# An attention-and-network megakernel: loads spread over three places of a slot, one masked query moved to ScalarE, five network groups turned by 32x32 blocks ahead of time

## The chip, the cores and the metric

The kernel runs on one core of a Trainium2 chip, in float32 throughout. The metric is the time of one execution on the device in microseconds; the median of several executions is compared. TensorE (PE in the profile, its weight loads PEld) does the matrix products, VectorE (DVE) and ScalarE (ACT) the elementwise work, GpSimd (POOL) what is left of it, and SyncE (SP) issues nearly all DMA transfers, one after the other, from one queue.

## The reference, cut to what matters

There are 16 sequences of 256 tokens with 256 features, and 16 contexts of the same shape. Each sequence goes through three attentions with 16 heads of 16 features, and then a network:

```python
# layer 0: cross-attention between RMS norms
q, k, v = rms(x) @ Wq, rms(ctx) @ Wk, rms(ctx) @ Wv
x = rms(x + softmax(q k' / 4, masked) v @ Wo)
# layer 1: causal self-attention with rotary embedding, layer 2: the same, not causal, with k, v from ctx
h = layernorm(x)
q, k = rope((h @ wq + bq) / 4), rope(h @ wk + bk)
x = x + softmax(q k', causal) v @ wo + bo
# layer 3
x = x + gelu(layernorm(x) @ fc1 + b1) @ fc2 + b2      # 256 -> 1024 -> 256
```

## The kernel before

**Slots.** The 48 attentions (16 sequences x 3 layers) are done one after the other, in an order written out by hand: the digits of `ORDER` (L31) are the layers. One attention is a *slot*. Inside slot i the kernel does the scores, exponentials and value products of attention i, block by block (`scores`, L538; `values`, L574), and in between pieces of other attentions: the q, k and v projections of attention i+1, the division and projection of attention i-2, the finish of i-3, the norms of i+2. A slot of layer 0 or 2 has four blocks; a causal slot (layer 1) has three, since the part above the diagonal is left out. Which piece stands where is written out in the loop at L983 to L1102; the program records instructions in that order, and each engine runs its own in order. Semaphores are the only link between engines.

In each block PE does the scores (L551), the value products of the block before (L590) and one 256-column projection (L329 for q and k, L341 for v and for the output). PE turns without a pause if everything that it reads is there: qm and kT of the next attention at the slot's boundary, the exponentials `pt` a block later.

**q and k.** For the layers 1 and 2, `q` (L474) adds the bias on ScalarE (L461), then VectorE does a shuffle (L465), two products (L469), a sum (L485) and two products with a 0/1 mask (L487): `qm` holds q twice, once with the even heads blanked out and once with the odd ones. `k` (L505) takes the same steps and ends with the sum into `kT` (L510). In a causal slot the k of the next attention follows on VectorE right behind its q; in the others the inversion of the softmax sums stands between them.

**The way of the value products.** `take` (L604) copies them from PSUM and sends them to DRAM (`hop<-av`), once for each half. `end` (L610, in block 0 of the next slot) sends the second half and fetches the sums and the values in another layout (`sums<-hop`, `oT<-hop`). `invert` (L622, block 1) takes reciprocals on VectorE (L627), and spreads them over partitions through DRAM (`inv_hop<-sums`, `inv<-inv_hop`). `divide` (L639, block 0 of the slot after) multiplies by them (L641). All of it is issued by SP in order, so that whatever stands ahead of a transfer on SP, or waits there, holds it up.

**Loads.** A layer-0 attention needs four transfers of 256 KB (x, y and both transposed: `cur`, `y`, `xT`, `yT`), issued in the slot three before it; there are 11 such slots (i = 3, 5, 7, 11, 14, 17, 21, 24, 29, 31, 33). `load_next` (L976) issues two of them in block 0, behind the transfers of `end`, and two in block 1, behind those of `invert`. Where no layer 0 is due, one weight matrix is issued at each of the two places while there are any.

**Turning.** A normalised sequence is needed with features on partitions. Either PE does it (`turn_ps`, L282: four 128x128 transposes into PSUM, then a copy), or `pieces_out` (L431) has VectorE transpose 32x32 blocks (L436) and writes them to DRAM, and `pieces_in` (L445) reads them back in four transfers. 23 of the attentions use the second way, 9 the first; the result is `hT`, with runs of 32 tokens.

**The network.** It handles two sequences at a time: eight groups (`Mlp`, L709), each with seven products of 512 features by Strassen-like sums for the first layer (`up`) and seven for the second (`down`). The loop at L1115 interleaves `up` of group g+1 with `down` of group g, and prepares group g+2: `stats`, `norm`, `keep` (adds a bias on POOL), `turn` on PE between `down(2)` and `down(7)` (L1156), with a copy to SBUF by ScalarE (L729), and `mix` (L748, four differences on VectorE). The PSUM tile `X` of `up` is used by four products in turn, and `add_sum` (L779) has to read it before the next.

Of the kernel before, what the change touches and what calls it, by code (L numbers as in the profile page):

```python
# [8 lines left out]
F32 = mybir.dt.float32  # L9
# [64 lines left out]
def xattn_kernel(  # L74
# [217 lines left out]
    def turned(src):  # L292
# [7 lines left out]
        return t  # L300

    def all_tokens(src, k, like=None):

        if len(src.shape) == 3:
            return src[:, k], like
        if like is not None:
            like = like.rearrange("p (c q i) -> p c q i", c=NC, i=32)
        return src[:, :, k].rearrange("p q c i -> p c q i"), like
# [40 lines left out]
    class Att:  # L349
# [81 lines left out]
        def pieces_out(self):  # L431

            self.norm()
            t = work.tile([P, 4, KC, NC, 32], F32, tag="a", name="turn")
            for k in range(KC):
                nc.vector.transpose(  # L436
                    t[:, :, k].rearrange("p g c i -> p c g i"),
                    self.xn[:, :, k * P : (k + 1) * P].rearrange("p c (g j) -> p c g j", j=32),
                )
            self.turn_hop = dram.tile([P, 4, KC * NC * 32], F32, tag="turn", name="turn_hop")  # L440
            nc.sync.dma_start(
                out=self.turn_hop, in_=t.rearrange("p g k c i -> p g (k c i)")
            )

        def pieces_in(self):  # L445

            self.hT = turn_tile()
            hop = self.turn_hop.rearrange("(q j) g f -> g j q f", j=32)
            for g in range(4):
                nc.sync.dma_start(  # L450
                    out=self.hT[32 * g : 32 * g + 32].rearrange("p q k c i -> p q (k c i)"),
                    in_=hop[g],
                )
            self.kvT = self.hT if self.layer == 1 else yTs[self.b]
# [18 lines left out]

        def q(self):  # L474
            ps = by_feature(self.hT, self.w, 0)
            self.qm = work.tile([P, KC, 2, S], F32, tag="qm", name="qm", bufs=2)
            if self.layer == 0:
                rq = self.rq.unsqueeze(1).to_broadcast([P, KC, S])
                for i in range(2):
                    nc.vector.scalar_tensor_tensor(  # L480
                        self.qm[:, :, i, :], ps, parity[i], rq, ALU.mult, ALU.mult
                    )
                return
            a, u = self.rotated(ps, 0)
            nc.vector.tensor_tensor(a, a, u, ALU.add)  # L485
            for i in range(2):
                nc.vector.tensor_scalar(self.qm[:, :, i, :], a, parity[i], None, ALU.mult)  # L487

# [220 lines left out]
    class Mlp:  # L709
# [11 lines left out]
        def keep(self):  # L721
            for x in self.xs:
                add_bias(x, R_FC2)

        def turn(self, copy=nc.scalar.copy):
            self.hT = self.pool.tile([P, KC, 2, S], F32, tag="qm", name="hT3")
            for i, xn in enumerate(self.xns):
                ps = turn_ps(xn)
                copy(self.hT[:, :, i, :], ps.rearrange("p (k s) -> p k s", s=S))  # L729

        def mix(self, tag="av", bufs=None):

            b = self.hT
            if tag == "av":
# [9 lines left out]
            for o, x, y in (  # L744
                (t1, b[:, 0, 1], b[:, 0, 0]), (t2, b[:, 1, 1], t1),
                (t3, b[:, 1, 1], b[:, 0, 1]), (t4, b[:, 1, 0], t2),
            ):
                nc.vector.tensor_tensor(o, x, y, ALU.subtract)  # L748

        def up_product(self, n, banks, a, b, first):  # L750
            for c in range(4):
                nc.tensor.matmul(  # L752
                    banks[c // 2][:, (c % 2) * S : (c % 2 + 1) * S],
                    lhsT=a[:, c * P : (c + 1) * P], rhs=b,
                    start=(first and c % 2 == 0), stop=True, skip_group_check=True,
                )
# [38 lines left out]
        def up(self, n):  # L795
            b, ts = self.hT, getattr(self, "ts", None)
            if n == 1:
                self.X = psS.tile([P, 2, 512], F32, tag="S", name="upX")
                self.X = [self.X[:, i] for i in range(2)]
                self.up_product(1, self.X, up_a(0, 0), b[:, 0, 0], True)  # L800
                self.keep_or_add(0, 0, self.X)
# [8 lines left out]
            elif n == 2:  # L810
                w = [dense_ps() for _ in range(2)]
                self.up_product(2, w, up_a(0, 1), b[:, 1, 0], True)
                self.keep_or_add(0, 0, w)
# [3 lines left out]
            elif n == 3:  # L817
                self.up_product(3, self.Z, up_s[2], b[:, 1, 1], False)
# [119 lines left out]
    with tc.manual_schedule():  # L938
# [36 lines left out]

        def load_next(i):  # L976
            n = 2 if i > 1 and ahead is not None and ahead.layer == 0 else int(i > 2)
            for t, w in due[:n]:
                nc.sync.dma_start(out=t, in_=w)
            del due[:n]  # L980

        turns = turned_ahead()
        for i in range(N_ATT):  # L983
# [4 lines left out]
            if i > 1 and ahead is not None and ahead.layer == 0:  # L988
                due[:0] = batch(ahead.b)


# [3 lines left out]
            for n in range(len(a.blocks)):  # L995
# [8 lines left out]
                if n == 0:  # L1004
# [9 lines left out]
                    do(turns.get(i - 1), "pieces_in")  # L1014
                    load_next(i)
                    if late:
# [13 lines left out]
                    if i == N_ATT - 1:  # L1030
                        mlps[0].turn(nc.vector.tensor_copy)
                        mlps[0].keep()
                    do(i + 1, "q")
                elif n == 1:

                    if a.causal:
                        do(i + 1, "k")
                    if last is not None:
# [76 lines left out]
        for g in range(B // 2):  # L1115
            this = mlps[g]
            ahead, next_but_one = (mlps[i] if i < B // 2 else None for i in (g + 1, g + 2))

# [472 lines left out]
```

## Time and profile before

| | |
|---|---|
| Median of 3 executions | 944.01 us (943.09 to 948.07) |
| Profiled execution | 935.7 us, its span 933.8 us |
| Granted TensorE clock | 0.999 |
| PE busy in the span | 920.2 us (99%) |
| DVE busy | 679.2 us (73%) |
| ACT busy | 533.2 us (57%) |
| POOL busy | 314.0 us (34%) |
| Attention, 89 to 708 us | PE 613.9 of 619 us |
| Network, 742 to 929 us | PE 186.97 of 187 us, DVE 122.49, ACT 73.62 |

Busy time of PE comes from modelled ends of pipelined products, so it is not a proof that PE runs at its peak; a delay shows best in the start of one stretch of products against the next. A row of the timeline has the start, the length, the engine with its line, the operation, output and inputs, shape and number; square brackets tell how long the engine was idle before it and what ended that. "SPq" is SP's issue of a transfer; its length is the time of issuing alone.

### The profile page before, as it was taken

The page shows a single profiled execution, that of the slowest core. Times are in us where ns is not written, and L with a number is a line of the kernel's source. Part 1 is how long each engine was busy: PE and PEld are TensorE (multiplying, and loading weights), DVE is VectorE, ACT ScalarE, POOL GpSimd, SP SyncE. Part 2 cuts the span into 40 slices and gives each one's busy share as a digit, 9 for nine tenths or more (in the row PEclk, how much of TensorE's full clock was granted, in tenths as well). Part 3 has the DMA queues.
Part 4 walks back from the last instruction along what each step waited for, and adds up shares of the span by engine and source line. Part 5 has one row for each costly group of instructions (what it writes and reads, how often), then busy time and mean ns, then how long its engine had stood idle before and what let it go on. Part 6 is the DMA issues. An engine that isn't in the chain of part 4 may idle for free.

```text
span 933.8 us, 29304 instructions
## 1 busy us (share of the span) xinstructions
PE 920.2 (99%) x12266; PEld 540.2 (58%) x12266; DVE 679.2 (73%) x1486; ACT 533.2 (57%) x749; POOL 314.0 (34%) x503
## 2 busy tenths in 40 slices
PE   8999999999999999999999999999999999999997
PEld 4444444445454544454454445455444799999997
DVE  4458677886878787868966878897887566667663
ACT  4666655766666665756656666666666634344440
POOL 4213543324444464443533434344033121122200
PEclk9999999999999999999999999999999999999999
DMA  9434454454334343432435433223222100000001
GB/s 297 155 100 126 128 170 136 132 159 125 124 106 144 94 129 98 152 111 84 141 121 157 132 106 98 90 86 102 92 76 82 36 24 23 20 4 24 24 24 48
DMA packets 115550, 95.26 MB, mean 102 GB/s; under 512 B 23498, under 2 KB 112210, under 8 KB 115410
## 3 DMA queue, kind: packets, MB, share of 16 engines
q1 hardware_dynamic: 114722, 92.77, 31.8%
q8 instruction: 98, 1.61, 0.7%
q10 hardware_dynamic: 688, 0.54, 0.2%
q14 instruction: 42, 0.34, 0.1%
HBM read 57.08 MB, written 36.20 MB: 100 GB/s over the span
## 4 chain that ended last, share of the span: by engine, by line
PE 78%; DVE 11%; DMA 5%; issue 2%; SPq 2%; POOL 2%; ACT 1%; DVEq 0%
PE S L551 15%; PE A L590 14%; PE d L341 13%; PE d L329 13%; PE upX L752 6%; PE A L850 5%; PE downZ L850 3%; PE upZ L752 3%; DVE u L469 2%; PE d L850 2%; DVE a L469 2%; PE d L752 2%; DVE u L465 1%; PE d L286 1%; DMA hop<-av 1%
## 5 line engine op out<-in xcount | busy, mean ns | idle before, releaser
L562 ACT ACTIVATE pt<-S 128x1024 f32<-128x1024 f32 x224 | 217.3, 1022 | 135.3 <-PE S L551 135.0
L551 PE MATMUL S<-qm,kT 32*128 32x512 f32 (+1 forms) x1536 | 202.8, 599 | 4.1 <-DVE kT L510 3.6
L590 PE MATMUL A<-pt,va 128*32 128x256 f32 (+1 forms) x3072 | 191.2, 367 | 1.3 <-POOL pt L569 0.7
L590 PEld LDWEIGHTS A<-pt,va 128*32 128x32 f32 x3072 | 80.5, 109 | 157.0 <-issue 92.7
L562 ACT ACTIVATE pt<-S,sy 128x1024 f32<-128x1024 f32 x128 | 135.7, 1111 | 50.8 <-PE S L551 50.5
L569 POOL TENSOR_SCALAR_AFFINE_SELECT pt<-pt 128x512 f32<-128x512 f32 x128 | 90.7, 725 | 147.5 <-ACT pt L562 146.6
L551 PEld LDWEIGHTS S<-qm,kT 32*128 32x128 f32 x1536 | 62.8, 183 | 76.0 <-issue 41.2
L317 POOL TENSOR_TENSOR cur<-cur,bias 128x512 f32<-128x512 f32 x48 | 68.7, 1438 | 56.5 <-DVE xn L271 56.5
L461 ACT ACTIVATE a<-d,qk_bias 128x256 f32<-128x256 f32 x128 | 53.8, 471 | 52.5 <-PE d L329 31.1
L329 PE MATMUL d<-hT,sa 128*32 128x256 f32 x1024 | 61.1, 379 | 0.0
L246 POOL TENSOR_SCALAR r_ln<-bmv 128x2 f32<-128x2 f32 x48 | 15.3, 318 | 118.0 <-DVE bmv L265 116.5
L469 DVE TENSOR_TENSOR u<-u,turn 128x512 f32<-128x512 f32 x64 | 52.2, 816 | 0.0
L469 DVE TENSOR_TENSOR a<-a,turn 128x512 f32<-128x512 f32 x64 | 49.8, 777 | 2.2
L641 DVE TENSOR_TENSOR oT<-oT,inv 128x512 f32<-128x512 f32 x48 | 39.2, 818 | 14.2 <-DMA inv<-inv_hop 13.0
L607 DVE COPY av<-A 128x512 f32<-128x512 f32 x47 | 32.2, 684 | 22.7 <-PE A L590 22.3
L465 DVE STREAM_SHUFFLE u<-a 128x512 f32<-128x512 f32 x64 | 47.4, 741 | 0.0
L790 ACT ACTIVATE g<-g,fb 128x256 f32<-128x256 f32 x96 | 41.0, 499 | 11.1 <-DVE g L779 11.1
L329 PEld LDWEIGHTS d<-hT,sa 128*32 128x32 f32 x1024 | 33.2, 110 | 22.0 <-issue 0.2
L246 POOL TENSOR_SCALAR r_o<-ms_o 128x2 f32<-128x2 f32 x16 | 3.9, 242 | 122.3 <-DVE sq L254 112.7
L650 DVE TENSOR_TENSOR cur<-d,cur 128x512 f32<-128x512 f32 x32 | 21.6, 676 | 29.0 <-PE d L341 29.0
L271 DVE TENSOR_SCALAR xn<-cur,bmv,r_ln 128x256 f32<-128x256 f32 x96 | 41.5, 481 | 0.8 <-POOL r_ln L247 0.8
L845 DVE TENSOR_TENSOR g<-g,g 128x512 f32<-128x512 f32 x64 | 40.9, 681 | 0.0
(148 smaller groups left out, 1556.0 us busy)
## 6 DMA issues: line engine op xcount, KB each, us to landing
hop<-av SPq DMA_DIRECT2D x96, 256.0 KB
oT<-hop SPq DMA_DIRECT2D x96, 128.0 KB
inv<-inv_hop SPq DMA_DIRECT2D x96, 128.0 KB
turn_hop<-turn SPq DMA_DIRECT2D x23, 256.0 KB
hT<-turn_hop SPq DMA_DIRECT2D x92, 64.0 KB
xT<-in_xt SPq DMA_DIRECT2D x16, 256.0 KB
cur<-in_x SPq DMA_DIRECT2D x16, 256.0 KB
yT<-in_yt SPq DMA_DIRECT2D x16, 256.0 KB
```

What stands on the lines that cost most here:

```text
L317: nc.gpsimd.tensor_tensor(t, t, bias_sb[:, row : row + D].unsqueeze(1).to_broadcast([P, NC, D]), ALU.add)
L329: nc.tensor.matmul(o, lhsT=w[:, k, at + t * P + j : at + t * P + j + 32], rhs=tokens, start=(k == 0), stop=(k == KC - 1), skip_group_check ...
L341: nc.tensor.matmul(ps[j : j + 32, c * D : (c + 1) * D], lhsT=some_tokens(src, k, c, j), rhs=w[:, k, at : at + D], start=(k == 0), stop=(k ...
L461: nc.scalar.activation(a[:, t], ps[:, t], AF.Identity, bias=bias[:, t : t + 1])
L465: nc.vector.stream_shuffle(u.rearrange("p t s -> p (t s)"), a.rearrange("p t s -> p (t s)"), SWAP)
L469: nc.vector.tensor_tensor(t, t, table.unsqueeze(1).to_broadcast([P, KC, S]), ALU.mult)
L551: nc.tensor.matmul(ps[:, j, 2 * m * u : 2 * m * (u + 1)] .rearrange("p (i s) -> p i s", i=2), lhsT=self.kT[r, t, kc * P : (kc + 1) * P], r ...
L562: nc.scalar.activation(pt[:, :, :w], ps[:, :, :w], AF.Exp, scale=scale)
L569: nc.gpsimd.affine_select(out=diag, in_=diag, compare_op=ALU.is_ge, fill=0.0, base=0, pattern=[[0, 2], [0, 2], [1, P]], channel_multiplier=-1,
L590: nc.tensor.matmul(self.av[32 * r : 32 * r + 32, i, q0:S], lhsT=self.va[:, kc, 8 * t + 2 * r + i, :], rhs=pts[r // 2][:, r % 2, i * m : (i ...
L752: nc.tensor.matmul(banks[c // 2][:, (c % 2) * S : (c % 2 + 1) * S], lhsT=a[:, c * P : (c + 1) * P], rhs=b, start=(first and c % 2 == 0), s ...
L850: nc.tensor.matmul(ps[:, c, :], lhsT=a[f // 2][:, f % 2, c * P : (c + 1) * P], rhs=b[:, f, :], start=(first and c == 0 and f == 0), stop=True,
```

## The change

It has three parts.

- `load_next` is called at three places instead of two: at the very start of a slot (ahead of the scores of block 0, so ahead of `end` on SP's queue), in block 1 behind `invert` as before, and in the last block. Where a layer 0 is due, two transfers go at the first place and one at each of the others (before: two and two). Where none is due, one weight matrix each at the first and the second (before: the same number, the first of them behind `end`).
- `q` can leave out the second of its two mask products. It does so if the current attention is causal; the product is then done by ScalarE, as an activation Copy with the mask as its scale, behind the two bias activations of k in block 1. Only next attentions of layer 1 or 2 have such a product, so that it concerns five causal slots (i = 21, 28, 38, 40, 42).
- The 32x32 way of turning becomes a pair of functions, and the network's groups 3 to 7 use it: statistics, norm and VectorE transposes of group g+3 in iteration g, writing to DRAM behind `down(3)`, and the reading back in iteration g+1. Groups 0 to 2 are turned by PE as before, now with a copy into the same layout. All products and differences that read this `hT` read it in runs of 32.

Instruction by instruction, PE loses 40 transposes and is otherwise unchanged; ScalarE loses ten copies and gains five activations; VectorE loses five mask products and gains 20 transposes, and statistics and norms move; POOL is unchanged; SP gains 10 writes and 40 reads in the network.

```diff
+    def pieces_out(xn):
+        t = work.tile([P, 4, KC, NC, 32], F32, tag="a", name="turn")
+        for k in range(KC):
+            nc.vector.transpose(
+                t[:, :, k].rearrange("p g c i -> p c g i"),
+                xn[:, :, k * P : (k + 1) * P].rearrange("p c (g j) -> p c g j", j=32),
+            )
+        hop = dram.tile([P, 4, KC * NC * 32], F32, tag="turn", name="turn_hop")
+        nc.sync.dma_start(out=hop, in_=t.rearrange("p g k c i -> p g (k c i)"))
+        return hop
+
+    def pieces_in(t, hop):
+        for g in range(4):
+            nc.sync.dma_start(
+                out=t[32 * g : 32 * g + 32].rearrange("p q k c i -> p q (k c i)"),
+                in_=hop.rearrange("(q j) g f -> g j q f", j=32)[g],
+            )
...
-        def q(self):
+        def q(self, both=True):
...
-            for i in range(2):
-                nc.vector.tensor_scalar(self.qm[:, :, i, :], a, parity[i], None, ALU.mult)
+            nc.vector.tensor_scalar(self.qm[:, :, 0, :], a, parity[0], None, ALU.mult)
+            self.rotated_q = a
+            if both:
+                nc.vector.tensor_scalar(self.qm[:, :, 1, :], a, parity[1], None, ALU.mult)
+
+        def second_mask(self):
+            if self.layer > 0:
+                nc.scalar.activation(
+                    self.qm[:, :, 1, :], self.rotated_q, AF.Copy, scale=parity[1]
+                )
...
+        def new_hT(self):
+            t = self.pool.tile([P, 2, 4, KC, NC, 32], F32, tag="qm", name="hT3")
+            self.hT = [t[:, i] for i in range(2)]
...
+        def pieces_out(self):
+            self.hops = [pieces_out(xn) for xn in self.xns]
+
+        def pieces_in(self):
+            self.new_hT()
+            for t, hop in zip(self.hT, self.hops):
+                pieces_in(t, hop)
...
-        def load_next(i):
-            n = 2 if i > 1 and ahead is not None and ahead.layer == 0 else int(i > 2)
+        def load_next(i, n, later):
+            if not (i > 1 and ahead is not None and ahead.layer == 0):
+                n = later if i > 2 else 0
...
                 due[:0] = batch(ahead.b)
+            load_next(i, 2, 1)
...
                     do(turns.get(i - 1), "pieces_in")
-                    load_next(i)
...
-                    do(i + 1, "q")
+                    if i + 1 < N_ATT:
+                        att(i + 1).q(both=not a.causal)
                 elif n == 1:
                     if a.causal:
-                        do(i + 1, "k")
+                        do(i + 1, "k", "second_mask")
...
-                    load_next(i)
+                    load_next(i, 1, 1)
...
                     do(due_turn, "turn")
+                    load_next(i, 1, 0)
...
-            if next_but_one is not None:
+            if g == 0:
                 next_but_one.stats()
             if ahead is not None:
                 ahead.ups(5, 6)
                 this.sum_a(2)
+            if g > 0 and next_but_one is not None:
+                next_but_one.keep()
+                next_but_one.pieces_in()
...
-            if next_but_one is not None:
+            if g == 0:
                 next_but_one.norm()
                 next_but_one.keep()
+            if third is not None:
+                third.stats()
...
             this.down(2)
+            if g == 0:
+                next_but_one.turn()
             if next_but_one is not None:
-                next_but_one.turn()
                 next_but_one.mix()
...
             this.down(7)
+            if third is not None:
+                third.norm()
             this.down(3)
+            if third is not None:
+                third.pieces_out()
             this.down(4)
```

More of the change, by code (lines that the diff above doesn't have):

```diff
@@ L300, in turned, with by_groups @@
         return t
+    def pieces_out(xn):
[14 more added lines that the diff above has]
+            )
+    def by_groups(t):
+        return t.rearrange("p (c q i) -> p c q i", c=NC, i=32)
     def all_tokens(src, k, like=None):
@@ L306, in all_tokens @@
         if like is not None:
-            like = like.rearrange("p (c q i) -> p c q i", c=NC, i=32)
+            like = by_groups(like)
         return src[:, :, k].rearrange("p q c i -> p c q i"), like
@@ L433, in pieces_out @@
             self.norm()
[L434 to L443, printed above, removed]
+            self.hop = pieces_out(self.xn)
         def pieces_in(self):
             self.hT = turn_tile()
[L448 to L453, printed above, removed]
+            pieces_in(self.hT, self.hop)
             self.kvT = self.hT if self.layer == 1 else yTs[self.b]
@@ L723, in keep, with part @@
                 add_bias(x, R_FC2)
+        def new_hT(self):
+            t = self.pool.tile([P, 2, 4, KC, NC, 32], F32, tag="qm", name="hT3")
+            self.hT = [t[:, i] for i in range(2)]
         def turn(self, copy=nc.scalar.copy):
-            self.hT = self.pool.tile([P, KC, 2, S], F32, tag="qm", name="hT3")
-            for i, xn in enumerate(self.xns):
+            self.new_hT()
+            for t, xn in zip(self.hT, self.xns):
                 ps = turn_ps(xn)
-                copy(self.hT[:, :, i, :], ps.rearrange("p (k s) -> p k s", s=S))
+                copy(
+                    t.rearrange("p q k c i -> p (k c) q i"),
+                    ps.rearrange("p (k q i) -> p k q i", q=4, i=32),
+                )
+        def pieces_out(self):
+            self.hops = [pieces_out(xn) for xn in self.xns]
+        def pieces_in(self):
+            self.new_hT()
+            for t, hop in zip(self.hT, self.hops):
+                pieces_in(t, hop)
+        def part(self, k, i):
+            return all_tokens(self.hT[i], k)[0]
         def mix(self, tag="av", bufs=None):
-            b = self.hT
+            b = self.part
             if tag == "av":
@@ L744, in mix @@
             for o, x, y in (
-                (t1, b[:, 0, 1], b[:, 0, 0]), (t2, b[:, 1, 1], t1),
-                (t3, b[:, 1, 1], b[:, 0, 1]), (t4, b[:, 1, 0], t2),
+                (t1, b(0, 1), b(0, 0)), (t2, b(1, 1), t1),
+                (t3, b(1, 1), b(0, 1)), (t4, b(1, 0), t2),
             ):
+                o, y = (t if len(t.shape) == 4 else by_groups(t) for t in (o, y))
                 nc.vector.tensor_tensor(o, x, y, ALU.subtract)
@@ L751, in up_product @@
             for c in range(4):
+                o = banks[c // 2][:, (c % 2) * S : (c % 2 + 1) * S]
                 nc.tensor.matmul(
-                    banks[c // 2][:, (c % 2) * S : (c % 2 + 1) * S],
+                    o if len(b.shape) == 2 else by_groups(o),
                     lhsT=a[:, c * P : (c + 1) * P], rhs=b,
@@ L795, in up @@
         def up(self, n):
-            b, ts = self.hT, getattr(self, "ts", None)
+            b, ts = self.part, getattr(self, "ts", None)
             if n == 1:
@@ L799, in up @@
                 self.X = [self.X[:, i] for i in range(2)]
-                self.up_product(1, self.X, up_a(0, 0), b[:, 0, 0], True)
+                self.up_product(1, self.X, up_a(0, 0), b(0, 0), True)
                 self.keep_or_add(0, 0, self.X)
@@ L811, in up @@
                 w = [dense_ps() for _ in range(2)]
-                self.up_product(2, w, up_a(0, 1), b[:, 1, 0], True)
+                self.up_product(2, w, up_a(0, 1), b(1, 0), True)
                 self.keep_or_add(0, 0, w)
@@ L817, in up @@
             elif n == 3:
-                self.up_product(3, self.Z, up_s[2], b[:, 1, 1], False)
+                self.up_product(3, self.Z, up_s[2], b(1, 1), False)
                 self.add_sum(1, 0, self.Z)
@@ L1116, in xattn_kernel @@
             this = mlps[g]
-            ahead, next_but_one = (mlps[i] if i < B // 2 else None for i in (g + 1, g + 2))
+            ahead, next_but_one, third = (
+                mlps[i] if i < B // 2 else None for i in (g + 1, g + 2, g + 3)
+            )
             if g == 0:
```

## The prediction

> **What bounds the kernel now.** I read the page's engine totals first, then PE's own waits, then the starts of PE's products in the timeline, and only there the other engines.
>
> ```profile
> span 933.8 us, 29304 instructions
> PE 920.2 (99%) x12266; PEld 540.2 (58%) x12266; DVE 679.2 (73%) x1486; ACT 533.2 (57%) x749; POOL 314.0 (34%) x503
> PE   8999999999999999999999999999999999999997
> ...
> 742.00:929.00 187.00, 186.97 (x1346) 175.44 (x1344) 122.49 (x261) 73.62 (x164) 30.85 (x36) 1.00 0.07 22
> ...
> PE S L551 <- DVE kT L510: 3.6, 8, 0.9
> PE A L590 <- POOL pt L569: 0.7, 3, 0.2
> ```
>
> PE is full. The fourth line is the table by stages for the network (length, then busy time of PE, PEld, DVE, ACT, POOL): 186.97 of 187 us. The last two are PE's waits between 80 and 708 us, the attentions: only 4.3 us in all by this view. So a gain can come from two things alone: products that PE no longer does, and the few places where it stands. The chain of waits names DMA and VectorE for a tenth and more of the span, but PE runs beside them; I don't use its shares.
>
> Since the ends of products are modelled, I measured the standing by starts. A causal slot takes 12.70 us from its first scores to those of the next where nothing waits (19, 26, 31, 33, 35 without a turn). Five take 13.13 or 13.14, four others 13.56 to 13.77 (5, 7, 9, 23). Slots 6 and 22 take 16.64 and 16.29 where their kind takes 15.63. These are the places to look at.
>
> **Part 1: 40 transposes fewer on PE.** In the network, in order of time:
>
> ```profile
> 808.76 1.04 PE L286 MATMUL d<-ident,xn 128*128 128x128 f32 x8
> 809.45 1.07 ACT L729 COPY hT<-d 128x512 f32<-128x512 f32 x2 [5.49 <-PE d L286]
> 809.63 1.95 PE L850 MATMUL A<-fc,g 128*128 128x128 f32 x16
> 810.56 0.42 DVE L748 TENSOR_TENSOR ts<-hT 128x256 f32<-128x256 f32 x1 [1.18 <-ACT hT L729]
> ```
>
> From the start of a group's eight transposes to the next product: 809.63 - 808.76 = 0.87 us, with PE full before and after. Five groups: **-4.4 us**. The ten ScalarE copies lie beside PE and bring nothing. Products that read hT in runs of 32 cost the same: with this layout 379 ns (d<-hT,sa) against 379 and 384 (yT, xT).
>
> What it adds must stay hidden. VectorE gets four transposes a group at 424 ns (row L436), 1.7 us; statistics and norm only move. A group lasts 25.6 us (from 752.63 to 829.35, the same downZ three groups on), and VectorE goes from 122.49/187 = 66% to some 72% there. Its order matters more. In the times of the trace before, with `mix` out of the way, the sum that ends `down(7)` could be done at 786.45. Behind it now stand the norm 1.7 us (2.3 beside POOL's bias sum), an end 0.4, the transposes 1.7, a begin 0.4 and two sums 2.8: 7.0 to 7.6 us, to 793.5 or 794.1. The first add_sum, which waits for `up(2)`, began at 795.84: 1.7 us of cover at the least, and then 0.17 and 1.04 us of idle time ahead of the next two. It costs nothing while these 2.9 us hold. Where they don't, the next to suffer is `up(4)`, which needs X read: add_sum ended 799.72, `up(4)` began 799.89, so all further delay is PE's.
>
> SP: ten transfers a group (8 reads at 0.47 us of issue, 2 writes), in a queue that has two stores there. The transposed group is needed by `mix` one iteration later, seven `up` (1.73 each) and four `down` (1.78): 19 us. In the attentions, by the semaphores, a write of turn_hop landed 2.0 to 5.8 us after issue, and the four reads by 5.6 us after the first's issue; with twice the reads that makes some 13 us.
>
> Here the Trainium skill speaks against the change: "VectorE: DVE Perf Modes", section "Rules for kernel authors", sends a 128x128 transpose to TensorE if PSUM will do, and the section on three transpose paths puts a plain strided copy at 19 times a proper DMA transpose. If the reads paid 19 times 5.6 us, an estimate of 106 us, each of five groups would come 80 us late: +400. The row says 5.6 us, as each run moved is 128 floats and only the blocks' insides are turned, on VectorE. I take the row.
>
> **Part 2: the mask.** Slot 42, the last of the five, PE, then VectorE, then ScalarE:
>
> ```profile
> 643.39 1.91 PE L341 MATMUL d<-sao,oT 128*32 128x256 f32 x32
> 645.67 1.14 PE L551 MATMUL S<-qm,kT 32*128 32x512 f32 x8 [0.37 <-DVE kT L510]
> ...
> 640.99 1.52 DVE L487 TENSOR_SCALAR qm<-a,vec 128x512 f32<-128x512 f32 x2
> 642.44 0.71 DVE L465 STREAM_SHUFFLE u<-a 128x512 f32<-128x512 f32 x1
> 644.51 1.01 DVE L510 TENSOR_TENSOR kT<-a,u 128x512 f32<-128x512 f32 x1
> ...
> 640.27 0.84 ACT L461 ACTIVATE a<-d,qk_bias 128x256 f32<-128x256 f32 x2 [0.76 <-PE d L329]
> 643.09 1.94 ACT L562 ACTIVATE pt<-S 128x1024 f32<-128x1024 f32 x2 [1.98 <-PE S L551]
> ```
>
> VectorE runs through from the masks to kT, which ends at 645.52; the scores start 0.15 us later. The two masks take 1.52 us, so the second gives 0.76. PE is late by 0.43 (13.13 against 12.70), in all five slots. ScalarE does the mask instead at 641.11, where the sum it reads has been ready since 640.95, and stands idle till 643.09; its nearest row is the copy 128x512 of L607, 0.59 us: it ends by 641.8 and delays no exponential. So **5 x 0.43 = -2.1 us**; the other 0.3 us of each stay with VectorE. The ends: -2.2, and 0 if something else, then, holds the scores (kT would be early by 0.3, less than one operation drawn out beside POOL, which the sum of 1.01 against 0.69 shows).
>
> **Part 3: the loads.** Two loads leave the place ahead of `inv_hop`, one leaves that ahead of the first `hop`. VectorE in slot 6, then SP in slots 21 and 22:
>
> ```profile
> 110.74 0.95 DVE L641 TENSOR_TENSOR oT<-oT,inv 128x512 f32<-128x512 f32 x1 [2.26 <-DMA inv<-inv_hop]
> 115.85 0.35 DVE L627 RECIPROCAL sums<-sums 128x32 f32<-128x32 f32 x1 [0.52 <-DMA sums<-hop]
> 118.32 0.69 DVE L510 TENSOR_TENSOR kT<-a,u 128x512 f32<-128x512 f32 x1
> ...
> 343.29 0.46 SPq L979 DMA_DIRECT2D xT<-in_xt  x1
> 343.79 0.47 SPq L979 DMA_DIRECT2D yT<-in_yt  x1
> 344.36 0.92 SPq L608 DMA_DIRECT2D hop<-av  x2
> 350.16 0.56 SPq L615 DMA_DIRECT2D sums<-hop  x1
> ```
>
> In slot 6 VectorE stands for inv, then for the sums, and PE's next scores come 1.01 us late. The inv_hop that this inv needs landed 3.97 us after its issue, with `cur` and `y` just ahead; at 340.50, with none ahead, it took 1.42. Cost of the old place: 2.5 us and 1.05 us of issue. Against it, the two now go ahead of the second `hop`. A queue of four transfers of 256 KB landed at 111.47, 112.14, 112.93 and 113.61, so 0.7 us each: hop, and all behind it, is up to 1.4 us later where SP reaches the loads only just before `end`, as in slots with a late turn_hop. Where SP is ahead, after a four-block slot, they land before it and cost nothing. In slot 6 inv_hop landed at 106.07 and the reads of hT ahead of it at 104.76, so inv can be about 1 us earlier, of which I keep 0.7, since a weight now stands ahead of its second hop (+0.7 on the sums). Slots 7 and 9 stand because POOL's masks of pt (L569) wait behind the norm of a VectorE that is late from the slot before: 0.7 and 0.4. Slots 22 and 23 (0.66 and 1.07) follow slot 21, where the mask's spare 0.3 us helps too, while xT, hop, yT, hop are still one after the other: 0.5 together. **-2.3 us**; ends +3 (1.4 us in two or three slots with no cover) and -4.7, all of 6, 7, 9, 22 and 23. Slot 5 stays: VectorE waited for no transfer ahead of it.
>
> **The sum.** 4.4 + 2.1 + 2.3 = 8.8 us off the profiled execution, 935.7 to 926.9. Its span and what lies around it shrink by the same; the median of the runs is 8.3 us above the profiled one for reasons that the profile doesn't show, so I take the difference: 944.0 - 8.8 = **935.2**.
>
> **Rivals.**
> - *The loads bring nothing* (what leaves inv_hop's way comes into hop's): 944.0 - 6.5 = 937.5. For it: slot 22's queue is the same four transfers. Against: slot 6.
> - *All stands caused by transfers go*: 944.0 - 6.5 - 4.7 = 932.8. For it: one late inv explains slots 6 and 7 alike. Against: structural waits, as in slot 5.
> - *VectorE becomes the bound in the network*: POOL's bias sums, now beside the transposes and sums, stretch them (one norm took 1.36 us instead of 0.40 beside L317); beyond the cover of 2.9 us each lost us is PE's. At 1 us a group, 5 us: 942.5, no change.
> - *Slower*: the loads at the slot's start hold up the second hop in all 11 load slots, and the reciprocal, ahead of k on VectorE in four-block slots, passes it to kT. 11 x 1.4 = 15.4, less 6.5: 953. It decides from eight slots paying in full. Against: kT is late in but two load-bound slots now, so that most have room.
>
> **How the numbers follow.** Half a per cent, 4.7 us, is about what a measurement here can tell from nothing: faster is below 939.3. Chances: as worked 0.52, loads nothing 0.25, all stands 0.10, VectorE's bound 0.08, slower 0.05. Faster: nearly all of the first three, less 0.05 for losses in between: 0.82; no change 0.13; slower 0.05. The likeliest's own range is 932 to 938.5; over the cases 930.5 to 941.
>
> **What would show it.** L286 x60 instead of 100, and the network's groups 24.7 us apart instead of 25.6; if they stay, look for idle VectorE ahead of L779 and PE waiting for g. Slots 21, 28, 38, 40, 42 at 12.70 and the wait of S for kT below 1.6 us; ScalarE's five Copies before 128x1024 exponentials without delay. In slots 6 to 9 and 22 to 23, inv_hop landing within 2 us and the idle time ahead of L641 (13.0 us in all) halved; if the idle time ahead of L626 and L627 grows by as much, the first rival holds. Wrong would be the whole if slots that stood at their least now stand longer.

## The result and the profile after

The changed kernel takes 934.89 us (median of 12 executions, 930.77 to 938.71) against 942.50 us (12 executions, 937.54 to 948.07) for the kernel before on the same chips: ratio 0.9922, 95% interval 0.9898 to 0.9946. The prediction was 935.2.

Executions of one and the same program differ here by up to 14 us, and the two profiled ones lie at opposite ends: 935.7 us for the kernel before, below all its timed ones, and 938.7 for the changed kernel, its longest. So the spans went from 933.8 to 936.7 us while the medians fell by 7.6. The two traces can be compared place by place, but not by their totals, until it is known which places vary by themselves.

The page of the changed kernel (totals, and PE by slices), then PE's own waits in its attentions (engine, tile and line waited for: us, times, longest), then the network's seven groups by stage (window; length; busy us of PE, PEld, DVE, ACT, POOL with the number of instructions; clock; DMA share; GB/s):

```profile
span 936.7 us, 29330 instructions
PE 918.8 (98%) x12226; PEld 536.5 (57%) x12226; DVE 679.6 (73%) x1501; ACT 530.8 (57%) x744; POOL 310.8 (33%) x503
PE   8999999999999999999999899999999999999997
```

```profile
PE S L566 <- DVE kT L525: 4.0, 4, 2.7
PE A L605 <- POOL pt L584: 1.6, 5, 0.8
```

```profile
759.70:920.95 161.25, 161.25 (x1132) 152.02 (x1131) 115.03 (x253) 60.41 (x136) 25.02 (x32) 1.00 0.17 55
```

PE is as full as before. The same seven groups took 165.62 us before:

```profile
752.47:918.09 165.62, 165.62 (x1173) 156.36 (x1171) 109.84 (x233) 65.79 (x146) 28.35 (x32) 1.00 0.07 22
```

One slice of the attentions has an 8 where the page before had a 9, and scores wait for kT four times, once for 2.7 us.

**The network**, with the changed kernel's groups of instructions by line (all transposes of PE in the program; those of VectorE in the network) and its timeline where PE's transposes used to be:

```profile
L286 PE MATMUL d<-ident,xn 128*128 128x128 f32 x60 | 9.1, 283 | 0.0
```

```profile
L306 DVE STREAM_TRANSPOSE turn<-xn 128x256 f32<-128x256 f32 x20 | 7.1, 405 | 0.0
```

```profile
790.53 1.95 PE L886 MATMUL A<-fc,g 128*128 128x128 f32 x16
792.31 1.95 PE L886 MATMUL downZ<-fc,g 128*128 128x128 f32 x16
...
795.89 1.89 PE L788 MATMUL upX<-hT,fc 128*128 128x256 f32 x8
```

Product follows product at 1.79 us, with no transposes between. The interval from one group's first downZ to the next went from 25.46 to 24.60 us (once from 25.78 to 24.91) wherever a group is no longer turned by PE, five times: -0.87 each on average, 4.37 us in all.

**The mask.** Slot 42, PE, then VectorE, then ScalarE:

```profile
651.39 1.91 PE L364 MATMUL d<-sao,oT 128*32 128x256 f32 x32
653.23 1.14 PE L566 MATMUL S<-qm,kT 32*128 32x512 f32 x8
```

```profile
648.97 0.74 DVE L493 TENSOR_SCALAR qm<-a,vec 128x512 f32<-128x512 f32 x1
...
651.73 0.69 DVE L525 TENSOR_TENSOR kT<-a,u 128x512 f32<-128x512 f32 x1
```

```profile
648.27 0.84 ACT L468 ACTIVATE a<-d,qk_bias 128x256 f32<-128x256 f32 x2 [0.76 <-PE d L352]
649.03 0.72 ACT L500 ACTIVATE qm<-a,vec 128x512 f32<-128x512 f32 x1
651.03 1.94 ACT L577 ACTIVATE pt<-S 128x1024 f32<-128x1024 f32 x2 [1.27 <-PE S L566]
```

kT ends at 652.42, 0.8 us ahead of the scores, which now follow the projection at once. The slot is 12.70 us long, and so are 21, 28, 38 and 40 (before 13.13 or 13.14). ScalarE's mask ends 1.27 us before the exponential that follows.

**The loads.** Slot 6, VectorE, the lines that the prediction showed of before:

```profile
109.71 0.70 DVE L656 TENSOR_TENSOR oT<-oT,inv 128x512 f32<-128x512 f32 x1 [0.98 <-issue]
...
116.24 0.35 DVE L642 RECIPROCAL sums<-sums 128x32 f32<-128x32 f32 x1 [1.61 <-DMA sums<-hop]
...
118.71 0.69 DVE L525 TENSOR_TENSOR kT<-a,u 128x512 f32<-128x512 f32 x1
```

inv is awaited for 0.98 us where it was 2.26 (the profile names nothing that ended this wait, but by the semaphores the second read of inv landed at 109.63), and the sums for 1.61 where it was 0.52. By the semaphores the sums landed 13.39 us into the slot, against 13.24 before, and kT begins 2.56 us behind that landing in both traces: 15.95 us into the slot, against 15.80. So kT hung on the sums, not on inv, already before the change. The slot is 16.80 us long, not 16.64: nothing gained. In this execution slots 8, 9, 12, 13, 16, 34 and 35 are also longer than in the profile before, by 10 us together. My first reading was that the new places of the loads do this.

### The profile page after: what moved, and what is told of

Same layout as the page of the kernel before. It is cut to its first block, busy times and chain, and to the rows that moved or that the text cites. A ratio compares the mean times of both kernels' runs of the same rounds, so it can differ in the third digit from the quotient of the medians.

```text
span 936.7 us, 29330 instructions
## 1 busy us (share of the span) xinstructions
PE 918.8 (98%) x12226; PEld 536.5 (57%) x12226; DVE 679.6 (73%) x1501; ACT 530.8 (57%) x744; POOL 310.8 (33%) x503
## 3 DMA queue, kind: packets, MB, share of 16 engines
q8 instruction: 98, 1.61, 0.7%
## 4 chain that ended last, share of the span: by engine, by line
PE 76%; DVE 9%; DMA 8%; SPq 2%; issue 2%; POOL 2%; ACT 0%; ACTq 0%; DVEq 0%; POOLq 0%
PE S L566 15%; PE A L605 14%; PE d L364 13%; PE d L352 12%; PE upX L788 6%; PE A L886 5%; DMA hop<-av 5%; PE downZ L886 3%; PE upZ L788 3%; PE d L886 2%; PE d L788 1%; DMA sums<-hop 1%; DMA inv_hop<-sums 1%; DVE u L476 1%; POOL pt L584 1%
## 5 line engine op out<-in xcount | busy, mean ns | idle before, releaser
L340 POOL TENSOR_TENSOR cur<-cur,bias 128x512 f32<-128x512 f32 x48 | 70.9, 1482 | 31.4 <-DVE xn L271 31.4
L810 ACT COPY g<-upX 128x512 f32<-128x512 f32 x28 | 15.0, 589 | 72.4 <-issue 67.5
```

The lines of the kernel that those rows point to most:

```text
L340: nc.gpsimd.tensor_tensor(t, t, bias_sb[:, row : row + D].unsqueeze(1).to_broadcast([P, NC, D]), ALU.add)
```

## The experiments

Times (us), and ratios against the kernel before as it ran beside each of them; `before_again` and `turn_dose` ran once, for their profiles (942.33 and 935.35 us):

| kernel | median | lowest to highest | ratio (95%) |
|---|---|---|---|
| `loads_only` | 939.23 | 936.78 to 948.67 | 0.9978 (0.9948 to 1.0009) |
| `net_mask` | 935.84 | 930.81 to 941.37 | 0.9936 (0.9909 to 0.9963) |
| `after_again` | 931.00 | 930.62 to 935.14 | 0.9896 (0.9858 to 0.9933) |
| `four_first` | 934.39 | 931.81 to 937.80 | 0.9919 (0.9894 to 0.9945) |
| `hop_wait_only` | 926.96 | 926.29 to 927.55 | 0.9872 (0.9845 to 0.9899) |
| `inv_wait_only` | 926.13 | 925.55 to 927.39 | 0.9860 (0.9834 to 0.9887) |
| `loads_in_waits` | 925.71 | 925.51 to 926.11 | 0.9839 (0.9794 to 0.9885) |
| `loads_by_act` | 925.60 | 924.45 to 926.15 | 0.9838 (0.9793 to 0.9884) |
| `before_in_waits` | 933.66 | 933.34 to 934.14 | 0.9947 (0.9927 to 0.9966) |
| `mask_in_waits` | 930.50 | 930.21 to 931.01 | 0.9902 (0.9871 to 0.9932) |

And the lengths of some slots in the profiled execution of each (us; a slot is counted from PE's first scores to those of the next; the least that any profile shows for the column stands in its head):

| kernel | 6 to 9 (56.66) | 12+13 (27.89) | 34+35 (28.33) | the five masked (63.50) | 22+23 (29.47) |
|---|---|---|---|---|---|
| before | 59.60 | 28.31 | 28.33 | 65.67 | 30.06 |
| `before_again` | 60.57 | 29.87 | 31.30 | 65.67 | 30.17 |
| `loads_only` | 60.35 | 27.89 | 28.33 | 65.66 | 30.13 |
| `net_mask` | 60.52 | 28.91 | 32.59 | 63.50 | 29.53 |
| after | 61.33 | 30.99 | 33.15 | 63.50 | 29.65 |
| `after_again` | 61.74 | 27.89 | 28.33 | 63.50 | 29.61 |
| `four_first` | 62.98 | 27.89 | 28.85 | 63.50 | 29.66 |
| `inv_wait_only` | 58.14 | 27.89 | 28.33 | 63.50 | 29.87 |
| `hop_wait_only` | 57.26 | 27.89 | 28.33 | 63.50 | 29.70 |
| `loads_in_waits` | 56.66 | 27.89 | 28.33 | 63.50 | 29.84 |
| `loads_by_act` | 56.66 | 27.89 | 28.33 | 63.50 | 29.47 |
| `before_in_waits` | 56.66 | 27.89 | 28.33 | 65.65 | 30.54 |
| `mask_in_waits` | 56.66 | 27.89 | 28.33 | 63.50 | 30.13 |

### The parts, and what varies by itself

`before_again` and `after_again` are the two kernels unchanged. `loads_only` is the kernel before with the new `load_next` and its three calls; `net_mask` is the changed kernel with the old ones:

```diff
-            load_next(i, 2, 1)
...
                     do(turns.get(i - 1), "pieces_in")
+                    load_next(i)
...
-                    load_next(i, 1, 1)
+                    load_next(i)
...
-                    load_next(i, 1, 0)
```

> The kernel before once more, for a second profile. If its profiled execution of 935.7 us was an early one of a wide spread, this one has a span some 5 us longer and stands in slots that stood at their least in the first, with no change in the network, groups 25.5 us apart. If stands belong to the program alone, the slots have the same lengths within 0.1 us.

> The changed kernel once more, to see which of its stands come back. If they belong to the order of the transfers, slots 8, 9, 12, 13, 16, 34 and 35 are longer again by about 0.9, 0.7, 2.0, 0.7, 0.9, 3.3 and 1.5 us than in the kernel before. If they come from transfers that happened to land late, the stands are in other slots, and the sum of the slots differs by some us. Ratio to the kernel before 0.992 in both cases.

> The change without its third part: loads at the two old places, the network's turning and the second mask as changed. The prediction's own sum: 4.4 + 2.1 = 6.5 us below the kernel before, ratio 0.993; slots 21, 28, 38, 40 and 42 at 12.70 us, groups of the network 24.6 us apart; slots 6, 7, 9, 22 and 23 stand as before. By the prediction it is 2.3 us slower than the whole change; if the loads bring nothing, it ties with it; if the three places cost what the one trace of the changed kernel shows (some 10 us), it is up to 8 us faster than the whole change.

> The kernel before with the loads alone at their three places. Prediction: 2.3 us below the kernel before, ratio 0.9976, with slots 6, 7, 9, 22 and 23 shorter. First rival: no change, ratio 1.000, idle time of VectorE moved from the inverse to the sums. If the stands in the trace of the changed kernel (slots 8, 9, 12, 13, 16, 34, 35) are the third part's own work: 5 to 10 us above, ratio 1.005 to 1.010, with these slots longer again.

The kernel before, profiled again, has a span of 940.5 us, and stands in slots 9, 12, 16, 34 and 35 for 0.73, 1.56, 0.89, 1.90 and 1.07 us more than in its first profile: five of the seven slots in which the changed kernel seemed to have lost. `after_again` keeps slots 9 and 16 but has 12, 13, 34 and 35 at their least. So these stands are not the change's work; they come and go, with either placing of the loads. My first reading fell. What stays in all profiles of either kernel is slots 6 to 9, 2.9 to 5.1 us above their least.

In the two profiles whose slot 34 stands longest, a part of the stand is not waiting. PE stood there for 2.74 us (changed kernel) and 2.50 us (`net_mask`), and the granted clock fell to 0.5 for 3.41 us, from 537.46 and from 524.24 on. In `net_mask`:

```profile
523.32 1.09 PE L605 MATMUL A<-pt,va 128*32 128x256 f32 x16 [2.50 <-DVE av L622]
524.21 3.60 PE L352 MATMUL d<-hT,sa 128*32 128x256 f32 x32
```

Such 32 products take 1.91 us elsewhere, so the lowered clock cost 1.7 us beyond the wait; in the changed kernel's profile it is the 1.51 us by which slot 35 is longer. In the other profiles PE never waits longer than 1.82 us from slot 3 on, and the clock is not lowered there. The mean clocks of the executions fit: of `net_mask`'s sixteen, those above 936 us have 0.995 to 0.997, those below 933 us 0.999 or 1.0. A part of the spread is thus the clock after long waits; how large a part is not measured.

The parts: `net_mask` is 0.9936 and `loads_only` 0.9978, so 6.0 and 2.1 us of 940.4 (4.6 and 1.2 between the medians), with 0 just inside the second interval; the lowest executions differ by 6.6 us (937.38 to 930.81) and 0.6 us. The network and the masks together are beyond doubt. The loads' part is not shown: besides this pair, the changed kernel is below `net_mask` by 0.9 us in its first twelve executions and by 4.8 us in the six of `after_again`, with overlapping intervals. Nor did anything come where it was meant to: of slots 6, 7, 9, 22 and 23 none is shorter by more than 0.02 us in `loads_only` than in the first profile of the kernel before.

Their mechanism can be read in VectorE's idle time, from 80 to 708 us, ahead of the two operations that wait for a hop. The columns after the bar are idle us and what ended it. First `net_mask` (loads at the old places), then `after_again` (new places):

```profile
L656 DVE TENSOR_TENSOR oT<-oT,inv 128x512 f32<-128x512 f32 x43 | 36.0, 837 | 12.1 <-DMA inv<-inv_hop 10.6 <-issue 1.5
L642 DVE RECIPROCAL sums<-sums 128x32 f32<-128x32 f32 x43 | 15.0, 349 | 16.7 <-DMA sums<-hop 12.1 <-POOL pt L584 3.5 <-issue 0.5
L641 DVE TENSOR_SCALAR sums<-sums 128x32 f32<-128x32 f32 x13 | 4.2, 327 | 12.9 <-DMA sums<-hop 12.8
```

```profile
L656 DVE TENSOR_TENSOR oT<-oT,inv 128x512 f32<-128x512 f32 x43 | 35.5, 825 | 6.5 <-DMA inv<-inv_hop 3.7 <-issue 2.8
L642 DVE RECIPROCAL sums<-sums 128x32 f32<-128x32 f32 x43 | 15.1, 350 | 23.6 <-DMA sums<-hop 20.0 <-issue 3.1
L641 DVE TENSOR_SCALAR sums<-sums 128x32 f32<-128x32 f32 x13 | 3.7, 285 | 15.9 <-DMA sums<-hop 15.9
```

inv: from 12.1 to 6.5 us in all (from 10.6 to 3.7 where the profile names inv). Sums, both lines together: from 24.9 to 35.9 us. That is the prediction's first rival in its own sign: what left the inverse's way came into the hop's, and VectorE stands no less.

### How much cover the network's VectorE has

```diff
-        for k in range(KC):
+        for k in list(range(KC)) * times:
```

with `times` = 1 for group 3, as it is, to 5 for group 7.

> The changed kernel, its transposes for the network done twice for group 4, three, four and five times for groups 5, 6, 7 (the same values written again), so that VectorE has 1.4, 2.8, 4.2 and 5.6 us more in iterations 1 to 4. The prediction's cover of 2.9 us: the intervals between those iterations stay 24.60 and 24.91, then grow by 1.3 and 2.7 us. Rival, VectorE is already the bound: each grows by its full 1.4, 2.8, 4.2, 5.6. Rival, PE has more room than the cover says: none grows.

The four intervals were 24.60, 24.90, 24.60 and 25.71 us: 0, 0, 0 and 1.1 us longer. The last iteration of the dose, VectorE and then PE:

```profile
865.05 6.63 DVE L306 STREAM_TRANSPOSE turn<-xn 128x256 f32<-128x256 f32 x20
...
875.52 1.27 DVE L815 TENSOR_TENSOR g<-g,upX 128x512 f32<-128x512 f32 x2
```

```profile
874.09 1.89 PE L788 MATMUL upZ<-hT,up_s 128*128 128x256 f32 x8
876.84 1.99 PE L788 MATMUL upX<-ts,fc 128*128 128x256 f32 x8 [0.86 <-DVE g L815]
```

Twenty transposes take 6.63 us, 5.2 more than the 1.41 of four, and PE's last upX starts 2.75 us after upZ instead of 1.73. It waits for the sum that reads X, as the prediction said the first sufferer would. Cover is thus about 4.1 us (5.2 - 1.1), not 2.9. In the changed kernel's own trace, idle time ahead of these sums is 2.23, 0.17, 1.04 and 0.37 us, 3.8 in all.

### Where a load costs nothing

After a hop is written, SP waits until it has landed before it can issue the reads; likewise after inv_hop. `loads_in_waits` issues the loads inside these two waits:

```diff
         def end(self, copy=nc.vector.tensor_copy, beside=lambda: None):
             self.take(1, copy)
+            beside()
...
-                        last.invert(lambda: do(i + 2, "send"))
+                        last.invert(lambda: (load_next(i, 2, 1), do(i + 2, "send")))
```

where `end` gets `load_next(i, 2, 1)` for `beside`, and has no other call of `load_next`. `four_first` calls `load_next(i, 4, 2)` at the start of the slot alone. `loads_by_act` keeps the three places and issues with `nc.scalar.dma_start`.

> The changed kernel with its loads inside two waits that SP has anyway: two behind the second hop and ahead of the reads of the sums, two behind inv_hop and ahead of the reads of inv (weights one and one). If a load costs by standing ahead of a small transfer that VectorE waits for (0.7 us each on its landing), both hop and inv_hop now have none ahead: landings of the second hop in load slots from 4.3 to 5.7 us down to some 3.5 to 4.5, inv_hop 2 us, VectorE's idle time ahead of the sums from 36 to 46 us down to 25, ahead of inv it stays below 6; the time 1 to 3 us below the changed kernel, ratio to the kernel before 0.988 to 0.990. If loads slow what is in flight wherever they stand, no difference to the changed kernel.

> The changed kernel with all four loads (or both weights) at the first place, ahead of the second hop. If each 256 KB ahead of it costs 0.7 us of landing, hop lands 1.4 us later than in the changed kernel in 11 slots, its sums come 8 us or more into the slot more often, and slots that follow a load slot stand: 3 to 8 us slower than the changed kernel, near the kernel before or above it. If landings are late at random, or the slots have room for it: within 1.5 us of the changed kernel.

> The changed kernel with the loads issued by ScalarE's queue at the same three places, so that SP issues them no more and they stand in another queue; the transfers and their bytes are the same. If SP's order is what makes hop and inv_hop late: VectorE's idle time ahead of the sums down to 20 to 25 us, time 2 to 4 us below the changed kernel, unless ScalarE's issues (some 0.5 us each, four in a load slot) hold up exponentials, which would show as PE waiting for pt. If the 16 DMA engines themselves are the limit: landings as in the changed kernel, time equal or slower.

Two loads in each wait: 925.71 us, 9 us below the changed kernel (5 us below `after_again`) and more than expected, and its four executions lie within 0.6 us of each other. SP's queue from slot 5 to slot 6, first of the changed kernel, then of `loads_in_waits` (the length is that of issuing):

```profile
91.30 0.50 SPq L1017 DMA_DIRECT2D cur<-in_x  x1
91.85 0.97 SPq L1017 DMA_DIRECT2D y<-in_y  x1
93.04 0.37 SPq L623 DMA_DIRECT2D hop<-av  x1
98.77 0.55 SPq L630 DMA_DIRECT2D sums<-hop  x1
...
102.61 0.43 SPq L644 DMA_DIRECT2D inv_hop<-sums  x1
105.77 1.22 SPq L650 DMA_DIRECT2D inv<-inv_hop  x2
...
110.44 0.42 SPq L623 DMA_DIRECT2D hop<-av  x1
114.13 0.55 SPq L630 DMA_DIRECT2D sums<-hop  x1
```

```profile
92.44 0.36 SPq L623 DMA_DIRECT2D hop<-av  x1
92.85 1.46 SPq L1018 DMA_DIRECT2D cur<-in_x  x1
94.36 0.46 SPq L1018 DMA_DIRECT2D y<-in_y  x1
96.20 0.55 SPq L631 DMA_DIRECT2D sums<-hop  x1
...
100.09 0.38 SPq L645 DMA_DIRECT2D inv_hop<-sums  x1
100.52 0.43 SPq L1018 DMA_DIRECT2D xT<-in_xt  x1
101.00 0.47 SPq L1018 DMA_DIRECT2D yT<-in_yt  x1
103.25 1.22 SPq L651 DMA_DIRECT2D inv<-inv_hop  x2
104.57 1.46 SPq L623 DMA_DIRECT2D hop<-av  x2
...
110.63 0.55 SPq L631 DMA_DIRECT2D sums<-hop  x1
```

The hop with two loads ahead of it is read 5.73 us after its issue; with two loads behind it, 3.76. (Not all of this is the two loads: with the same two ahead it is 4.89 us in `inv_wait_only`, below.) The inv_hop wait holds two loads and still ends after 3.16 us, no later than the changed kernel's 3.16. By the next slot's reading of the sums SP is 3.5 us ahead (110.63 against 114.13; the slot itself starts 0.6 us earlier). VectorE in slot 6 of `loads_in_waits`:

```profile
108.08 0.68 DVE L657 TENSOR_TENSOR oT<-oT,inv 128x512 f32<-128x512 f32 x1
...
113.42 0.34 DVE L643 RECIPROCAL sums<-sums 128x32 f32<-128x32 f32 x1
...
115.85 0.69 DVE L525 TENSOR_TENSOR kT<-a,u 128x512 f32<-128x512 f32 x1
```

No brackets: it waits for neither. kT begins 13.69 us into the slot instead of 15.95, and slots 6 to 9 are at 15.63, 12.70, 15.63 and 12.70.

`four_first` missed its expectation: four loads ahead of the hop cost no more than two ahead and two later, 934.39 us. So the delay of that one hop isn't the price by itself. Yet its profile, of its slowest execution, stands in slots 24, 25, 29 and 30 for 4.7 us more than the changed kernel's. `loads_by_act` gives 925.60: the same transfers, off SP's queue. PE's waits in the attentions are 0.5 us in all, so ScalarE's issues, mostly 0.37 us each, do no harm. The Trainium skill ("DMA: Bandwidth & Descriptors", section "Issuing engines are not separate DMA queues") says that issuing from several engines saves only the sequencer's time, as the transfers run on the same 16 engines anyway. That time is some 4 x 0.45 us of SP in each of 11 load slots, 20 us in all by an estimate from the lengths of issue; the run agrees in that no byte less was moved (100.5 MB in both), and the program is 5 to 9 us shorter. Whether SP's time or the place in SP's queue counts, this run doesn't tell apart.

### One wait or the other

`hop_wait_only` moves only the first two loads into hop's wait; `inv_wait_only` only the last two into inv_hop's.

> The changed kernel with only its first two loads moved, from the start of the slot to behind the second hop and ahead of the reads of the sums; the other two stay in block 1 and in the last block. If the hop's delay alone made the stands of slots 6 to 9, 12 and 34: second hop landings as with loads in both waits (3.6, 2.1 and 2.2 us in slots 5, 7 and 33), 925 to 927 us, 8 us below the changed kernel. If the loads between inv and the next first hop matter as well: 928 to 932 us, with slots 6 or 8 standing.

> The changed kernel with its first two loads still at the start of the slot and the other two behind inv_hop and ahead of the reads of inv. If the hop's delay is what counts: no gain, 933 to 936 us, second hop landings of 5 us in slots 5, 7 and 33 as in the changed kernel. If it is the loads in block 1 and in the last block: 925 to 928 us.

Both give nearly all of it, 926.96 and 926.13. The second was to gain nothing if the hop's delay counts: in it two loads still stand ahead of the hop, which in slot 33 lands 4.4 us after its issue (semaphores of the trace; 2.2 in `loads_in_waits`), and yet slots 34 and 35 stand at their least. So neither place is the culprit. Ordered by how many of a slot's four loads SP has to issue outside its waits, the times are: none 925.7 and 925.6, two 927.0 and 926.1, four 934.4 (`four_first`), 934.9 and 931.0 (changed kernel), 935.8 (`net_mask`). Where the four stand makes no difference that shows in the times; that two of them go does. The reading that fits all of these is that SP's round in the slots from 5 to 14 and from 29 to 34, a chain of hops each awaited in order, is about as long as the slots, so that SP gets to the next hop late.

The traces show this lateness. The second hop of a slot can be issued as soon as `av` is copied. In slot 6, first of the changed kernel, where that hop is SP's at 110.44 above, then of `loads_in_waits`:

```profile
105.52 0.67 DVE L622 COPY av<-A 128x512 f32<-128x512 f32 x1
```

```profile
104.93 0.69 DVE L622 COPY av<-A 128x512 f32<-128x512 f32 x1
105.65 0.37 SPq L623 DMA_DIRECT2D hop<-av  x1
```

SP is 4.26 us late in the one and 0.03 in the other. Summed over slots 5 to 35, it is late by 21.5 us in the changed kernel's profile and by 12.3 in `after_again`, by 19.7 in `four_first`, 11.6 in `net_mask`, 11.9 in `loads_only`, 9.7 and 10.9 in the two profiles of the kernel before; by 4.1 and 3.1 in `inv_wait_only` and `hop_wait_only`, 1.8 in `loads_by_act`, and by 0.9 to 1.0 in the three with loads in both waits, which is 0.03 per slot. In the changed kernel it is late by 2.9, 2.2, 2.1 and 1.9 us in slots 8, 12, 33 and 34, and `after_again`, in which slots 12, 34 and 35 stand at their least, is not late in 12, 33 and 34. So lateness is carried from slot to slot where the round has no spare time, and is made good once two loads are taken out of it. The when and why of a single late landing is not settled by these runs.

### Masks and network in a quiet setting

`before_in_waits` is the kernel before with both waits used; `mask_in_waits` has the second mask on ScalarE as well. Against `loads_in_waits`, the network alone is missing there.

> The kernel before (network and masks as before) with its loads inside the two waits. If the loads' part and the 6.5 us of the other two parts add up: 925.7 + 6.5 = 932.2 us, ratio 0.990 to 0.992, with slots 6, 7 and 9 at 15.63, 12.70 and 12.70 us and a narrow spread of its executions. If the masks' spare 0.3 us is needed for the gain in the slots: 934 us or more, with slots 22 and 23 or 7 and 9 standing.

> The kernel before with its loads inside the two waits and, of the other two parts, the second mask alone on ScalarE: in that quiet setting its worth stands apart from the network's. The prediction's term, 5 x 0.43 = 2.2 us: 933.66 - 2.2 = 931.5 us, and 5.8 us left for the network. With the slots behind the masked ones shorter too, by 0.7, 0.2 and 0.3 us in slots 22, 30 and 43 as the profiles with both parts have it: 933.66 - 3.4 = 930.3 us, and 4.5 us left for the network, which is its own term of 4.4.

933.66, 930.50, 925.71: with executions within 0.8 us of each other, the masks are worth 3.2 us and the network 4.8 us. The three ran on three chips; the spans of their profiles, 931.2, 928.5 and 923.8, give 2.7 and 4.7. The masks' profile shows where the rest of theirs is: five slots at 12.70 (2.15 us), and besides them slot 22 took 16.36 us instead of 16.77, 30 15.19 instead of 15.41, 43 16.22 instead of 16.53, 0.94 us together. Against these stands slot 16, which was 0.90 us longer in this profile; it is 13.29 or 14.18 in profiles of one and the same kernel. For the network, 4.4 us are in its own intervals; 0.28 us are in slot 22, which also varies by itself. And the kernel before gains 4.5 us of 938.15 by the medians (5.0 by the ratio, 0.9947) from its loads' places alone, with none of the change.

## Why the prediction was right, and where it wasn't

**The total was right, with one term too small and one that isn't shown, and partly by luck.** 944.0 - 8.8 was the forecast; the measured saving is 7.6 us (5.1 to 9.6 by the interval). By the runs it consists of 4.4 to 4.8 for the network, 2.7 to 3.2 for the masks, and a part of the loads that isn't told from nothing.

**Part 1, -4.4: right.** The intervals shrank by 0.87 us five times, and 4.8 us in the quiet setting. VectorE's order held as worked out, with more cover than counted: 4.1 us for 2.9. The first idle time is 2.23 us and not 1.7, and the 0.37 ahead of the fourth pair of sums was left out. The eight reads landed within 5.1 to 5.8 us of the first issue, not "some 13": they are issued 0.5 us apart and overlap, so that twice the reads didn't take twice the time. In the first such group they landed at 780.1 and were needed at 791.1. Of the +400 us that the rule of 19 times would have made nothing is in the trace, whose reads move runs of 128 floats. VectorE becomes the bound only from about 4.1 us more a group on.

**Part 2, -2.1: right in its places, a fifth to a third too small.** The five slots are as predicted to 0.01 us. "The other 0.3 us of each stay with VectorE" was the step that failed: slots 22 and 43, right behind masked ones, and 30, two behind one, became shorter by 0.94 us together, so VectorE's head start goes on into the slots behind. (For slot 22 the prediction said so itself, but counted it among the loads.) The part measured 2.7 to 3.2, outside the ends of -2.2 and 0. The wait of scores for kT was to fall below 1.6 us; it is 4.0 in the changed kernel's profile, 1.7 in its second and 0.4 in `loads_in_waits`: what is left of it goes when the loads do.

**Part 3, -2.3: not shown, and wrong at each of its slots.** inv did come earlier (2.26 to 0.98 us of idle time in slot 6), as worked out: the inv_hop that it needs landed 3.15 us after its issue where that had been 3.97, though not within 2. "Of which I keep 0.7" failed: kT did not wait for inv. The last wait ahead of it was the one for the sums, 0.52 us in the lines of before; the sums came 0.15 us later, and so did kT. Slots 6 and 7 did not get shorter, 9 was longer (14.29 for 13.56), 22 gained 0.41 by the mask in the quiet setting, and 23 is 13.76 or 13.77 in every profile. The error behind it is that each load was priced by the transfer just behind it, 0.7 us, and then credited where it left and debited where it went. What paid was taking loads out of SP's round. The rival "loads bring nothing" had the mechanism, and the symptom named for it, idle time ahead of L641 going to L626 and L627, is what came. "All transfer stands go, 4.7" was not what this change did. In the waits the same loads do end the stands of 6, 7 and 9, but not that of 23, which no run here moved. The rival of a slower kernel is refuted by `four_first`: even four loads ahead of the hop cost no more than the changed kernel.

**The base, and the luck.** The sum was taken off the median of three executions, 944.0, and not off the profiled one, 935.7, whose stands in slots 9, 12, 16 and 34 happened to be small or missing. The medians of the five sets of executions of the kernel before are 938.2 to 942.5; against the 942.5 that belongs to the result, the base was 1.5 us too high, and the masks and the network were put 0.6 to 1.5 us too low. Both put the forecast too high; the 2.3 us of the loads, which are not shown, put it too low. That these cancel to 0.3 us is luck.

## What to carry to other kernels

Where one engine issues transfers in order and waits for landings, a bulk load belongs behind the write whose landing is awaited and ahead of the read that awaits it, or in another engine's queue; counting the loads that stand outside such waits told more than pricing each by its neighbour. To credit an earlier transfer, ask first whether its wait is the one that ends last: here it was inv that came earlier and the sums that kT hung on. Before a stand in one profile is explained, a second profile of the same kernel shows which stands are the program's; a variant with a narrow spread is then the setting in which small parts can be weighed. And an engine's head start at the end of one stretch goes on to the next stretch: look for what was late there.

## What the runs showed of the hardware

- The spread of executions went with the order of transfers: 10.6 us between lowest and highest for `net_mask` (16 executions), 0.8 for `before_in_waits` (9) and 0.6 us for `loads_in_waits` (4), with the same transfers and nearly the same products.
- After PE had waited 2.50 and 2.74 us, the granted clock was 0.5 for 3.41 us; after waits of up to 1.82 us it stayed at 1.0.
- Eight reads of 64 KB in runs of 128 floats, issued 0.5 us apart, landed 1.8 to 3.8 us after their own issue. With two loads of 256 KB ahead, a hop of 256 KB was read 5.73 us after its issue, in another run 4.89; with the two behind it, 3.76.
- Four transposes of 32x32 blocks, 128x256 each, take 1.41 us in a row, twenty 6.63: one begins every 0.33 us, although each alone is 0.40 us long in the trace.
